# Moving vector work between the steps of a software pipeline: sums, gathering, statistics and one matrix product in a four-layer graph network

## The chip, the cores and the metric

The kernel runs on one core of one Trainium2 chip. The core has a matrix engine (PE, with its weight loads shown apart as PEld), a vector engine (DVE), an activation engine (ACT), GpSimd (POOL) and a queue engine for transfers (SP); they run at the same time and wait for each other through semaphores. The metric is the device time of one execution in microseconds (us). Three runs before the change took 1749.77, 1753.45 and 1761.13 us; the median, 1753.45 us, is the time to compare with.

## The reference

There are 128 small graphs of 64 nodes with 128 features each, and a weighted adjacency matrix `adj` of 64 x 64 for each graph. Four layers follow each other, and each is `x = layernorm(x + layer(x, adj))`.

Layers 0 and 1 are filter layers. For each edge they expand the distance into Gaussians, send them through a small network and multiply the result with the features of the neighbour, summed over the neighbours. Then come two dense layers with a shifted softplus (ssp) between them:

```python
# layer 0 (layer 1 differs in the Gaussians, the cut-off and the second ssp's place)
f_ij = jnp.exp(coeff * diff * diff)
y = x @ w_in2f
W = ssp(f_ij @ fw1 + fb1) @ fw2 + fb2
W = W * rcut[..., None]
agg = jnp.einsum('bjf,bijf->bif', y, W)
out = ssp(agg @ ow1 + ob1) @ ow2 + ob2
```

Layers 2 and 3 are graph convolutions: `norm_A @ (h @ W)` with a normalised adjacency matrix, two of them with elu in layer 2 and one with relu in layer 3.

## The kernel before

The adjacency matrices are sparse, so the kernel first sorts each graph's rows by their number of entries and packs the entries into slots of fixed sizes. This "gathering" is long: it finds the entries of each row with MAX8, FIND_INDEX8 and MATCH_REPLACE8 on DVE, and most of it runs beside layer 0, as the queue `early` (lines 1148 to 1155 and 1174).

**The main loop.** Two graphs make a pair; there are 64 pairs, and for two layers 128 turns `n`. Each turn is cut into three chunks of slots, `k` = 0, 1, 2, so the loop has 3 x 128 + 2 steps `i`. One step does, for three chunks at different stages:

- `filter_in` of this step's chunk: the product `px` on PE (L1708), then two activations into `h` on ACT (both L936).
- `filter_out` and `message` of the chunk of two steps ago: the products `pw` on PE (L1721), two of them in the only two buffers there are, and then two messages `m = (pw + bias) * g` on DVE (L1749). The next step's `pw` must wait for these two messages.
- `gather` of the chunk of one step ago: the product `pg` with the one-hot matrix on PE (L1734), and its copy `g` on ACT.
- when `k` = 0, the one-hot matrix of the turn (`hot`, L1693), one long DVE instruction.

**Sums.** After a turn's third message the generator `slot_sums` adds the slots of each row: seven reductions at L1773, each followed by a `yield`, and two at L1777 after them. The third message of a turn is made in the step with `k` = 1 of the next turn, so the sums stand in the steps with `k` = 2, 0 and 1 that follow, and have ended before that step's node work is placed.

**Node work.** Four pairs make a group (GS = 4). When a group's sums are done, its chain `node_after` is put into the queue `nodes`, and every step takes one piece of it. The pieces are: in layer 0 the share of the empty slots (`zero_share`), then the product `u` of the sums with the first dense matrix on PE (L1503); on ACT the activations Abs, Exp and Ln of `na`; on DVE `nh = max(u + bias, 0)` (L1511), `bk` (L1516) and the addition of `na` (L1519); the product `o` (L1523), its copy, the product `back` that restores the order of rows (L1532), the addition to x (L1536), and `layernorm` (L1354). A `yield True` says that a product has been put into PSUM; the rest of its piece then follows in the same step. In the layernorm BATCH_NORM_STATS2 and BATCH_NORM_AGGREGATE (L1359, L1360) run once for each of the four pairs on DVE, one small DVE instruction follows (L1362), and in the next step POOL makes the power and the scaling. In layer 1 the group's graph convolutions follow in one of two queues `convs`, eighteen steps or so each, with two further layernorms. Every full group comes in 12 steps; the last pairs of layer 1 are small groups with queues of their own, so that the end is short.

**Order.** Nothing is reordered later: `in_order` gives PE, ACT, DVE, POOL and SP the order in which the program names the instructions. On an engine everything in a step waits for what was named before it. In a step DVE has first the sums, then the gathering, the one-hot if `k` = 0, the node work, the first convolution's pieces as they come, and the messages.

The lines that drive it are

```python
        run(sums, 3)
        run(early, 9 if i < 18 else PACE if i < 3 * (NP - 8) else 7)
```

with PACE = 4 and NP = 64; `run(queue, n)` takes n pieces from a queue.

Of the kernel before, what the change touches and what calls it, by code (L numbers as in the profile page):

```python
# [601 lines left out]
def sparse_stack(ctx: ExitStack, tc: tile.TileContext, t: dict, out: bass.AP, flag):  # L602
# [14 lines left out]
    NP = NB // 2  # L617
    GS = 4
    PACE = 4
# [156 lines left out]
    def run(queue, n):  # L776

        held = None
        while queue and n:
            try:  # L780
                held = next(queue[0])
                n -= 1
            except StopIteration:
                queue.popleft()
        return held
# [139 lines left out]
    def act(out_, in_, func, **kw):  # L925
        nonlocal fence, latest, kind
        now = func == AF.Sin
        if kind is None or now != kind:
            fence = latest
            if not now:  # L930
                ctx_ = tc.issue_after(fence.ins) if fence is not None else nullcontext()
                with ctx_:
                    fence = nc.scalar.preload_act_table_set("natural_log_exp_and_others")
            kind = now
        with tc.issue_after(fence.ins) if fence is not None else nullcontext():
            latest = nc.scalar.activation(out_, in_, func, **kw)  # L936
        return latest
# [393 lines left out]
    def bank(name, n=GS):  # L1331
        ps = ps_n.tile([P, 512], F32, tag="n", name=name)[:, 0 : n * P]
        return ps, ps.rearrange("p (s c) -> p s c", s=n)

    def by_pair(v):
        return v.rearrange("p (s c) -> p s c", c=P)
# [11 lines left out]
    def once(name, n, q):  # L1348

        if n < GS and rings:  # L1350
            return tiled(name, n, q)
        return node.tile([P, GS * P], F32, tag=name, name=f"{name}_{q}", bufs=1)[:, 0 : n * P]

    def layernorm(y, dst, n, name):  # L1354

        stats = node.tile([P, GS, 6], F32, tag="st", name=f"st_{name}")[:, 0:n]
        mv = node.tile([P, GS, 2], F32, tag="mv", name=f"mv_{name}")[:, 0:n]
        for s in range(n):
            nc.vector.bn_stats(stats[:, s, :], y[:, s, :])  # L1359
            nc.vector.bn_aggr(mv[:, s, :], stats[:, s, :])  # L1360
        rstd = node.tile([P, GS], F32, tag="rs", name=f"rs_{name}")[:, 0:n]
        nc.vector.tensor_scalar(rstd, mv[:, :, 1], LN_EPS, None, ALU.add)  # L1362
        yield
        if n == GS:
            nc.gpsimd.tensor_tensor(rstd, rstd, neg_half[:, 0:n], ALU.pow)  # L1365
        else:
            act(rstd, rstd, AF.Ln)
            act(rstd, rstd, AF.Exp, scale=-0.5)
        for s in range(n):
            (nc.gpsimd if n == GS else nc.vector).tensor_scalar(  # L1370
                dst[:, s, :], y[:, s, :], mv[:, s, 0:1], rstd[:, s : s + 1],
                ALU.subtract, ALU.mult,
            )
        yield
# [81 lines left out]
    def zero_share(q, agg):  # L1456

        n = agg.shape[1]
        rows = zero_rows.pop(q)
        for b in range(2):  # L1460
            at = slice(b * A, (b + 1) * A)
            nc.vector.tensor_scalar(zblk[at, :, at], rows[at], 0.0, None, ALU.is_equal)
        yield
        _, ps = bank(f"zT_{q}", n)
        for s in range(n):
            nc.tensor.transpose(ps[:, s, :], zblk[:, s, :], ident)
        yield True
        zt = by_pair(once("zt", n, q))
        act(zt, ps, AF.Copy)
        yield  # L1470
        _, ps = bank(f"zs_{q}", n)
        y = feats[0, q]
        for s in range(n):
            nc.tensor.matmul(ps[:, s, :], lhsT=y[:, s, :], rhs=zt[:, s, :], start=True, stop=True)
        yield True
        nc.vector.scalar_tensor_tensor(agg, ps, zero_filter, agg, ALU.mult, ALU.add)
        yield
# [15 lines left out]
    def node_after(layer, q, agg):  # L1493


        w = layers[layer]
        name = f"{layer}_{q}"
        n = agg.shape[1]
        codes = node_codes.pop((layer, q))
        if layer == 0:  # L1500
            yield from zero_share(q, agg)
        u, _ = bank(f"u_{name}", n)
        nc.tensor.matmul(  # L1503
            u, lhsT=w["o1"], rhs=agg.rearrange("f s r -> f (s r)"), start=True, stop=True
        )
        yield True
        a = once("na", n, q)
        act(a, u, AF.Abs, bias=w["c1"])
        act(a, a, AF.Exp, scale=-1.0)
        h = once("nh", n, q)  # L1510
        nc.vector.tensor_scalar(h, u, w["c1"], 0.0, ALU.add, ALU.max)  # L1511
        yield
        act(a, a, AF.Ln, scale=0.5, bias=half)

        back = once("bk", n, q)
        nc.vector.tensor_scalar(back, codes, row[:, 0:1], None, ALU.is_equal)  # L1516
        back = by_pair(back)
        yield
        nc.vector.tensor_add(h, h, a)  # L1519
        yield  # L1520
        _, ps = bank(f"o_{name}", n)
        for s in range(n):
            nc.tensor.matmul(  # L1523
                ps[:, s, :], lhsT=h[:, s * P : (s + 1) * P], rhs=w["o2"], start=True, stop=True
            )
        yield True
        o = by_pair(once("no", n, q))
        act(o, ps, AF.Copy)
        yield
        _, ps = bank(f"back_{name}", n)  # L1530
        for s in range(n):
            nc.tensor.matmul(ps[:, s, :], lhsT=back[:, s, :], rhs=o[:, s, :], start=True, stop=True)  # L1532
        yield True
        y = by_pair(once("ny", n, q))
        xs = x_all[:, GROUPS[layer][q], :]
        nc.vector.tensor_add(y, ps, xs)  # L1536
        yield
        yield from layernorm(y, xs, n, name)
        if layer == 1:
            if n < GS:  # L1540
                yield from graph_convs(q)
            else:
                convs[q % 2].append(graph_convs(q))
# [241 lines left out]
    befores, nodes, convs, sums = deque(), deque(), (deque(), deque()), deque()  # L1785
# [36 lines left out]
    early = deque([gathering()])  # L1822
# [28 lines left out]
    for i in range(3 * N + 2):  # L1851
        n, k = divmod(i, 3)
        c, c1, c2 = None, *past
        run(sums, 3)
        run(early, 9 if i < 18 else PACE if i < 3 * (NP - 8) else 7)
        run(side, 1)
        run(stores, 1)
        if i == 3 * (NP + 5):
            assert not early and not side and not convs[0], "edges are still to be gathered"
            compacting.close()  # L1860
            rings.append(ctx.enter_context(tc.tile_pool(name="srings", bufs=4)))
            for q in (0, 1, *small_groups):
                group = GROUPS[1][q]
                blocks[q] = rings[0].tile(
                    [P, group.stop - group.start, P], F32, name=f"blocks{q}", bufs=1
                )
                nc.gpsimd.memset(blocks[q], 0.0)

            small[2] = by_pair(node.tile([P, GS * P], F32, tag="zt", name="small2", bufs=1))
            small[3] = zblk  # L1870
        if n < N:
            layer, p = pair_at(n)
            q = next(q for q, group in enumerate(GROUPS[layer]) if group.start <= p < group.stop)
            c = dict(
                id=f"{n}_{k}", n=n, k=k, s=p - GROUPS[layer][q].start, at=(layer, q), w=layers[layer],
                size=CHUNKS[layer][p // 8],
            )
            if k == 0:
                if n + GS < N:
                    ahead(n)  # L1880
                if n + 2 < N:
                    slot_data[n + 2] = loads(n + 2)
                if c["s"] == min(2, len(range(NP)[GROUPS[layer][q]]) - 1):
                    load_nodes(layer, q)
                if n > 0:
                    one_hot(n)
                if layer == 1 and c["s"] == 0 and q in last:
                    last[q].append(normals_of(q))
            filter_in(c)
        slot(nodes)  # L1890
        if k == 1 and befores:
            slot(befores)
        for queue in last.values():
            slot(queue)
        if c2 is not None:
            filter_out(c2)
            message(c2)
        if convs[0]:
            slot(convs[0])
        if k < 2 and n + 1 < N:  # L1900
            gaussians(n + 1, k)
        if c1 is not None:
            gather(c1)
        slot(convs[1])
        for queue in last.values():
            slot(queue)
        past = [c, c1]
# [53 lines left out]
```

## Time and profile before

| what | value |
|---|---|
| time, median of three | 1753.45 us |
| span of the profiled execution | 1760.8 us |
| PE busy | 1546.0 us, 88% |
| weight loads busy | 802.9 us, 46% |
| DVE busy | 1536.1 us, 87% |
| ACT busy | 1358.7 us, 77% |
| POOL busy | 737.7 us, 42% |
| one-hot matrices (L1693) | 128 of 1382 ns |
| reductions of the sums (L1773, L1777) | 896 of 411 ns, 256 of 368 ns |
| messages (L1749) | layer 0: 384 of 565 ns, layer 1: 384 of 628 ns |
| statistics (L1359, L1360) | 256 of 267 ns, 256 of 182 ns |
| product `u` in layer 1 (L1503) | 36 instructions of 692 ns |
| mean granted clock of PE | 0.957 |

"Busy" is the time in which an engine works on at least one instruction. The profile shows each instruction's start and length, and for an idle stretch before it, which engine's instruction ended it. In a list of waits a line reads: who waited, for whom, us in total, how many times, the longest. A timeline line reads: start in us from the span's beginning, duration, engine, line, operation, what is written and read, shapes, count, and in brackets the idle time before it and what ended it. The granted clock is the share of full speed that PE was given.

### The profile page before, as it was taken

How to read it: one execution, taken by the hardware profiler on the slowest of the kernel's cores; microseconds unless marked ns; L12 is line 12 of the kernel's file. 1: busy time of each engine (PE TensorE's matmuls, PEld its weight loads, DVE VectorE, ACT ScalarE, POOL GpSimd, SP SyncE). 2: the span in 40 equal slices, each digit the busy share in tenths (PEclk: the TensorE clock that was granted, in tenths of full speed). 3: DMA queues.
4: the chain of work that ended last, by engine and by line, in shares of the span. 5: the costliest groups of instructions: out<-in, count | busy, mean ns of one | idle time of the engine just before them, and what ended most of it. 6: DMA issues, size and time to landing. Idle time of an engine off the chain costs nothing.

```text
span 1760.8 us, 24324 instructions
## 1 busy us (share of the span) xinstructions
PE 1546.0 (88%) x6812; PEld 802.9 (46%) x6812; DVE 1536.1 (87%) x4485; ACT 1358.7 (77%) x1699; POOL 737.7 (42%) x1150
## 2 busy tenths in 40 slices
PE   1288999999989898989999989999899998999975
PEld 1133444444444444545445545455454554544444
DVE  6699899999999898888888889888898888989775
ACT  1287798888878787869999878878788787888731
POOL 2356454536556432335122354333444334534333
PEclk9998899999989898999999999999999999999986
DMA  4365456354545443336665445544454444555300
GB/s 147 84 156 130 107 127 155 106 143 105 147 108 138 108 121 94 106 82 150 153 144 121 118 108 139 121 115 113 108 134 112 117 110 103 134 125 120 75 1 21
DMA packets 112658, 202.86 MB, mean 115 GB/s; under 512 B 47214, under 2 KB 63872, under 8 KB 112384
## 3 DMA queue, kind: packets, MB, share of 16 engines
q1 hardware_dynamic: 99856, 185.24, 43.5%
q0 software_dynamic: 8080, 14.47, 2.8%
q10 hardware_dynamic: 4576, 1.49, 0.3%
q8 instruction: 56, 0.92, 0.2%
q14 instruction: 90, 0.74, 0.2%
HBM read 186.66 MB, written 14.45 MB: 114 GB/s over the span
## 4 chain that ended last, share of the span: by engine, by line
PE 47%; DVE 32%; DMA 7%; issue 5%; ACT 4%; POOL 2%; SPq 1%; DVEq 0%; ACTq 0%; POOLq 0%
PE pw L1721 17%; PE pg L1734 9%; PE px L1708 7%; DVE m L1749 7%; DVE agg L1773 6%; DVE hot L1693 4%; DMA w<-w_dram 2%; DMA d<-d_dram 2%; PE o L1523 2%; ACT h L936 2%; DVE st L1359 2%; PE y L1395 2%; PE back L1532 1%; DVE mv L1360 1%; DVE agg L1777 1%
## 5 line engine op out<-in xcount | busy, mean ns | idle before, releaser
L936 ACT ACTIVATE g<-pg 128x672 f32<-128x672 f32 (+12 forms) x384 | 299.4, 780 | 151.4 <-PE pg L1734 147.0
L936 ACT ACTIVATE h<-h,half 128x672 f32<-128x672 f32 (+13 forms) x385 | 351.2, 912 | 12.5
L1734 PE MATMUL pg<-hot,ys 64*128 64x336 f32 (+12 forms) x1536 | 351.2, 535 | 0.4 <-DVE hot L1693 0.3
L1773 DVE TENSOR_REDUCE agg<-m 128x16 f32<-128x240 f32 (+13 forms) x896 | 325.3, 411 | 2.5
L1721 PE MATMUL pw<-h,w_L_gnn_W2T 128*128 128x420 f32 (+5 forms) x768 | 310.3, 527 | 4.4 <-DVE m L1749 4.4
L1721 PE MATMUL pw<-h,w_L_gnn_fw 128*128 128x336 f32 (+6 forms) x768 | 279.7, 489 | 37.2 <-DVE m L1749 36.5
L1365 POOL TENSOR_TENSOR rs<-rs,neg_half 128x4 f32<-128x4 f32 x61 | 63.1, 1035 | 447.1 <-DVE rs L1362 447.0
L1749 DVE SCALAR_TENSOR_TENSOR m<-pw,c_L_gnn_b,g 128x420 f32<-128x420 f32 (+5 forms) x384 | 229.2, 628 | 19.6 <-PE pw L1721 13.3
L936 ACT ACTIVATE h<-px,c_L_gnn_b 128x840 f32<-128x840 f32 (+5 forms) x192 | 177.3, 924 | 61.3 <-PE px L1708 61.3
L1749 DVE SCALAR_TENSOR_TENSOR m<-pw,c_L_gnn_fb,g 128x336 f32<-128x336 f32 (+6 forms) x384 | 201.9, 565 | 25.0 <-PE pw L1721 24.1
L1708 PE MATMUL px<-d,fw 32*128 32x336 f32 (+6 forms) x768 | 169.9, 519 | 43.8 <-ACT d L936 29.9
L1734 PEld LDWEIGHTS pg<-hot,ys 64*128 64x128 f32 x1536 | 118.5, 189 | 181.7 <-ACT h L936 93.3
L1721 PEld LDWEIGHTS pw<-h,w_L_gnn_fw 128*128 128x128 f32 x768 | 139.1, 200 | 135.4 <-DVE m L1749 89.2
L1721 PEld LDWEIGHTS pw<-h,w_L_gnn_W2T 128*128 128x128 f32 x768 | 133.6, 194 | 134.7 <-DVE m L1749 40.9
L1693 DVE SCALAR_TENSOR_TENSOR hot<-j,row,w 128x1212 f32<-128x1212 bf16 (+12 forms) x128 | 176.9, 1382 | 11.1 <-DMA w<-w_dram 11.1
L936 ACT ACTIVATE h<-px,c_L_gnn_fb 128x672 f32<-128x672 f32 (+6 forms) x192 | 158.3, 825 | 15.3 <-PE px L1708 8.3
L1708 PE MATMUL px<-d,w1t 64*128 64x420 f32 (+5 forms) x768 | 169.4, 518 | 0.0
L936 ACT ACTIVATE d<-d,neg_off 128x1212 f32<-128x1212 f32 (+12 forms) x128 | 136.3, 1065 | 6.4 <-DMA d<-d_dram 6.4
L1708 PEld LDWEIGHTS px<-d,fw 32*128 32x128 f32 x768 | 60.1, 190 | 138.9 <-ACT h L936 44.6
L1008 POOL DMA_INDIRECT rows<-comb,goes x64 | 65.1, 1017 | 124.3 <-DMA rows<-comb,goes 92.7
L1008 POOL DMA_INDIRECT out_dram<-gz,at_row x56 | 62.8, 1122 | 105.1 <-DMA out_dram<-gz,at_row 95.9
L1370 POOL TENSOR_SCALAR x_all<-ny,mv,rs 128x128 f32<-128x128 f32 x124 | 97.0, 788 | 3.4
(255 smaller groups left out, 2297.0 us busy)
## 6 DMA issues: line engine op xcount, KB each, us to landing
d<-d_dram SPq DMA_DIRECT2D x32, 315.0 KB
w<-w_dram SPq DMA_DIRECT2D x32, 315.0 KB
d<-d_dram SPq DMA_DIRECT2D x32, 303.0 KB
w<-w_dram SPq DMA_DIRECT2D x32, 303.0 KB
w<-w_dram SPq DMA_DIRECT2D x32, 252.0 KB
j<-j_dram SPq DMA_DIRECT2D x32, 157.5 KB
j<-j_dram SPq DMA_DIRECT2D x32, 151.5 KB
d<-d_dram SPq DMA_DIRECT2D x16, 300.0 KB
```

The lines of the kernel that those rows point to most:

```text
L936: latest = nc.scalar.activation(out_, in_, func, **kw)
L1008: nc.gpsimd.indirect_dma_start(out=into, out_offset=bass.IndirectOffsetOnAxis(ap=at, axis=0), in_=rows, in_offset=None,)
L1359: nc.vector.bn_stats(stats[:, s, :], y[:, s, :])
L1365: nc.gpsimd.tensor_tensor(rstd, rstd, neg_half[:, 0:n], ALU.pow)
L1370: (nc.gpsimd if n == GS else nc.vector).tensor_scalar(dst[:, s, :], y[:, s, :], mv[:, s, 0:1], rstd[:, s : s + 1], ALU.subtract, ALU.mult,)
L1395: nc.tensor.matmul(ps[:, s, :], lhsT=xt[:, s * P : (s + 1) * P], rhs=w["win"], start=True, stop=True)
L1693: nc.vector.scalar_tensor_tensor(hots[n][:, 0:size], j[:, 0:size], near, wt[:, 0:size], ALU.is_equal, ALU.mult)
L1708: nc.tensor.matmul(ps[:, b, 0:n], lhsT=w["w1"][rows, :], rhs=d[rows, col : col + n], start=True, stop=True,)
L1721: nc.tensor.matmul(ps[:, 0 : c["size"]], lhsT=c["w"]["w2"], rhs=c["h"][:, b, :], start=True, stop=True)
L1734: nc.tensor.matmul(ps[:, b, 0:n], lhsT=y[rows, :], rhs=hots[c["n"]][rows, at], start=True, stop=True,)
L1749: nc.vector.scalar_tensor_tensor(messages[n][:, b, at], c["pw"][b][:, 0:size], c["w"]["b2"], c["g"][:, b, :], ALU.add, ALU.mult,)
L1773: nc.vector.tensor_reduce(av[:, :, :, r], both, AX.X, ALU.add)
```

## The change

The change removes and adds no computing. It shifts work between steps so that the step with the one-hot matrix (`k` = 0) has less other work on DVE, and so that a product isn't asked for in the step in which its input ends:

- of the sums' pieces, 1, 4 and 4 are taken when `k` is 0, 1, 2, where 3 were taken in each;
- of the gathering's pieces, 2, 5 and 5, where 4 were taken in each, in most of layer 0;
- in a layernorm of a whole group a `yield` stands after the second pair's statistics, so they are spread over two steps;
- in layer 1 a whole group's chain begins with a `yield`, so that `u` and all after it come one step later. In layer 0 `zero_share` stands there already.

```diff
@@ layernorm @@
         for s in range(n):
             nc.vector.bn_stats(stats[:, s, :], y[:, s, :])
             nc.vector.bn_aggr(mv[:, s, :], stats[:, s, :])
+            if s + 1 == GS // 2 < n:
+                yield
@@ node_after @@
         if layer == 0:
             yield from zero_share(q, agg)
+        elif n == GS:
+            yield
         u, _ = bank(f"u_{name}", n)
@@ the main loop @@
         n, k = divmod(i, 3)
         c, c1, c2 = None, *past
-        run(sums, 3)
-        run(early, 9 if i < 18 else PACE if i < 3 * (NP - 8) else 7)
+
+
+        run(sums, (1, 4, 4)[k])
+        run(early, 9 if i < 18 else (PACE - 2, PACE + 1, PACE + 1)[k] if i < 3 * (NP - 8) else 7)
         run(side, 1)
```

## The prediction

> **What bounds the kernel now.** I read the page first: busy shares, then the chain that ended last.
>
> ```profile
> PE 1546.0 (88%) x6812; PEld 802.9 (46%) x6812; DVE 1536.1 (87%) x4485; ACT 1358.7 (77%) x1699; POOL 737.7 (42%) x1150
> PE 47%; DVE 32%; DMA 7%; issue 5%; ACT 4%; POOL 2%; SPq 1%; DVEq 0%; ACTq 0%; POOLq 0%
> ```
>
> Two engines are equally busy and the chain changes between them, so hand-overs set the time. Next, busy time by stage. The timeline gives the borders: the first pair of messages (L1749) ends at 91 us, the last of layer 0 at 837, the last of layer 1 at 1702.
>
> ```profile
> 91.00:837.00 746.00, 681.08 (x2957) 336.92 (x2955) 684.89 (x2387) 619.62 (x816) 360.68 (x555) 0.95 0.49 123
> 837.00:1702.00 865.00, 810.19 (x3652) 427.61 (x3649) 751.76 (x1703) 709.85 (x829) 330.45 (x373) 0.98 0.49 116
> 1702.00:1760.80 58.80, 33.35 (x144) 25.35 (x142) 37.98 (x131) 8.56 (x31) 19.60 (x24) 0.67 0.05 16
> ```
>
> Columns are PE, PEld, DVE, ACT and POOL busy, then the granted clock and DMA. Layer 0 has 192 steps of 3.9 us with DVE 92% busy; layer 1 has 192 of 4.5 us with DVE 87%. DVE idles 61 us in layer 0 and 113 us in layer 1. DMA share is 0.49, no bound. Who waits, first in layer 0, then in layer 1:
>
> ```profile
> PE pw L1721 <- DVE m L1749: 36.5, 38, 3.6
> DVE m L1749 <- PE pw L1721: 23.6, 24, 3.9
> ```
>
> ```profile
> DVE nh L1511 <- ACT na L936: 37.6, 18, 3.0
> PE u L1503 <- DVE agg L1777: 36.3, 17, 3.3
> ```
>
> In layer 0, PE and DVE wait for each other around `pw` and the messages. In layer 1 one place dominates: PE waits for the last sums, and DVE then waits in `nh`. It recurs once a group; here, at 1208 us:
>
> ```profile
> 1207.82 0.69 DVE L1777 TENSOR_REDUCE agg<-m 128x8 f32<-128x272 f32 x2
> ...
> 1208.56 1.13 PE L1503 MATMUL u<-agg,w_L_gnn_Wd1T 128*128 128x512 f32 x2 [1.80 <-DVE agg L1777]
> ...
> 1209.73 0.69 ACT L936 ACTIVATE na<-u,c_L_gnn_bd 128x512 f32<-128x512 f32 x1 [1.00 <-PE u L1503]
> ...
> 1210.45 0.75 DVE L1511 TENSOR_SCALAR nh<-u,c_L_gnn_bd 128x512 f32<-128x512 f32 x1 [1.94 <-ACT na L936]
> ```
>
> Sums end, then `u`, then Abs, then `nh`: a serial loop through three engines, in which DVE, the fullest engine, is idle for 1.94 us and everything behind it on PE (`y`, `pw`) is late. From the ends of the message pairs in the timeline, the step with `u` takes 7.9 us on average where the mean is 4.5; DVE works 4.9 us in it.
>
> The other burst, in layer 0, is a step k = 0 with the one-hot and a whole layernorm's statistics:
>
> ```profile
> 506.76 1.26 DVE L1693 SCALAR_TENSOR_TENSOR hot<-j,row,w 128x1008 f32<-128x1008 bf16 x1
> 507.94 0.29 DVE L1359 BATCH_NORM_STATS2 st<-ny 128x6 f32<-128x128 f32 x1
> ...
> 509.66 0.17 DVE L1362 TENSOR_SCALAR rs<-mv 128x4 f32<-128x4 f32 x1
> 509.74 1.04 DVE L1749 SCALAR_TENSOR_TENSOR m<-pw,c_L_gnn_fb,g 128x336 f32<-128x336 f32 x2
> ```
>
> The messages stand behind 3 us of other work, and the next `pw` on PE then waited 1.89 us for them. Last, the clock before and at a `u` stall:
>
> ```profile
> 1140.00:1152.00 12.00, 10.52 (x53) 5.84 (x53) 9.79 (x25) 8.76 (x11) 0.20 (x1) 1.00 0.34 83
> 1152.00:1159.00 7.00, 5.60 (x14) 3.58 (x15) 2.54 (x6) 3.55 (x5) 5.04 (x6) 0.54 0.58 123
> ```
>
> The clock falls to 0.54 where PE stalls for `u` (its product starts at 1153.4). By the clock's record, layer 1 spends 27 us at half clock, 20.5 us of it in four places that begin within 1.1 us of a `u`; layer 0 spends 78.5 us so, for instance just after the burst at 510.9 us.
>
> **What the Trainium skill says.** "Perfetto Trace Analysis", Identifying the Most-Contended Engine, calls matmul busy time a bad measure and points to weight-load busy time. Agrees: PE 88% stands beside PEld 46%, so I treat DVE as the throughput bound and PE as the one whose stalls hurt. "PSUM — Partial Sum Buffer", PSUM bank collisions, has two engines kept off one bank and quadrant, reads included: that is why `nh` waits for Abs though both only read `u`. The 1.94 us agree. "TensorE: Matmul & The Clock Gate", Part 1, says the clock falls to half after a window of too little PE activity. Agrees with the 0.54. The same part, in its architectural detail, gives VectorE a strict first-in first-out queue: what stands ahead of the messages delays them. Agrees with the burst.
>
> **The change part by part.** It adds and removes no work: every matmul, activation and DVE instruction is still there once.
>
> (1) *Sums.* Nine reductions a pair (seven L1773, two L1777) stood 3, 3, 3 over k = 2, 0, 1; now 4, 1, 4. The step of the one-hot has two reductions fewer: 325.3 us / 896 = 0.36 us each, 0.7 us. The sums still end in k = 1.
>
> (2) *Gathering.* 4, 4, 4 becomes 2, 5, 5 nearly to layer 0's end. These are mostly MAX8, FIND_INDEX8 and MATCH_REPLACE8 of about 0.21 us: 0.4 us off k = 0.
>
> (3) *Statistics.* Four pairs of L1359 and L1360 take 1.72 us (507.94 to 509.66); 0.86 us moves on by a step. In layer 0 the statistics fall in k = 0, the second half now in k = 1.
>
> Together, in layer 0 (loads summed from the timeline): DVE has 4.3, 2.9 and 3.5 us in k = 0, 1, 2, mean 3.5. After: 4.3 - 0.5 (layer 0's reductions are shorter, 0.27 us) - 0.4 - 0.2 (0.86 once in four) = 3.2; 2.9 + 0.3 + 0.2 + 0.2 = 3.6; 3.5 + 0.3 + 0.2 = 4.0. The spread nearly halves. DVE's 23.6 us of waiting for `pw` is the gain available, and PE's 36.5 us its cause; between none and all of it, I take half: 12 us.
>
> (4) *`u` a step later in layer 1.* PE no longer waits for sums that ended a step ago. `nh` still waits for Abs, which on ACT stands behind the step's Exp and Ln, but four reductions (1.4 us) are ahead of it. The nearest row is layer 0, where sums are likewise long done at `u`: `nh` idles 11.4 us in 15 groups, 0.76 us each. Layer 1 idles 34.7 / 17 = 2.04 us. The difference, 1.28 us, times 15 full groups is 19 us. Bounds: zero, if the wait moves whole, and 35 us.
>
> (5) *Clock.* At half clock PE needs about 6.4 us for a layer 0 step that lasts 3.9 (3.2 us of matmuls at full speed, an estimate from start-to-start times in the timeline), so such stretches lose about 0.39 of their length: 30 us in layer 0. In layer 1 (8 us against 4.5) the four stalls lose 9 us. Part of that is the waits already counted. I take 8 and 5 us; bounds 0 and 39.
>
> (6) *What the delay costs.* The wait added is one of position: each node chain of layer 1 ends two steps later, each graph convolution takes two more. The chain then has 9 of a group's 12 steps (layer 0: 11), a convolution 20 of its 24, so neither queues. Three layernorms a group share two statistics buffers, each now held a step longer, about three steps of twelve; DVE waited for POOL here only 1.0 us. But two convolutions of four pairs run about four steps further into the tail of 58.8 us, whose own chain is the last pair's. Eight such pieces at 0.4 us, half of the DVE row of 0.6 to 0.7 us, partly in that chain's waits: +3 us, bounds 0 and 8.
>
> Sum: -12 - 19 - 8 - 5 + 3 = -41; 1753 - 41 = **1712 us**.
>
> **Rivals.** *The waits move.* DVE's total is unchanged and PE, ACT and DVE differ by little a step, so a stall removed at `u` returns at `nh`, `gy_hw` or `em`. For: DVE's small waits for PE in the convolutions (`gy_hw` 11.1, `em` 8.5, `gz` 8.2 us) are untouched. Against: `u` is one place with a cause of its own. A quarter of the gains, 11 us, less 3: 1745 us.
>
> *Slower.* Four reductions now stand ahead of everything else in k = 1 and k = 2, and in layer 1 the shifted pieces meet: the step two after the new `u` gets two activations' halves (1.3 us), half a statistics and the reductions, about 5.2 us on DVE. If PE stalls there 1.5 us a group in 16 groups, that is 24 us, with the tail at 8 and the gains of layer 0 at 12: 1753 + 24 + 8 - 12 = 1773 us. Against: layer 1 already has steps with 6.2 us of DVE work, and PE waits only 4.4 us for messages there.
>
> *More.* Nearly all of it: 20 + 30 + 25 = 75 us, 1678 us. For: stalls and half clock feed each other.
>
> **How the numbers follow.** Forecast 0.55, waits move 0.22, slower 0.12, more 0.11. One per cent is 17.5 us, so faster means below 1736. The forecast with its bounds falls there nine times in ten; so 0.49 + 0.02 + 0.11 gives faster 0.62, same 0.25, slower 0.13. The range is 1680 to 1760: it leaves out most of the slower case and the end of "more".
>
> **What would show it.** Right: `u` <- sums nearly gone in layer 1; `nh` <- Abs near 15 us; `pw` <- messages below 20 us in layer 0; fewer half-clock stretches, page clock from 0.957 to 0.97. The prediction is wrong if `nh` or the copies in the convolutions wait as long as `u` did, if half clock stays, or if the last stretch grows past 65 us.

## The result and the profile after

| what | before | after |
|---|---|---|
| time, median of four runs each | 1757.29 us (1749.77 to 1762.16) | 1710.61 us (1702.35 to 1715.96) |
| ratio after to before, 95% interval | | 0.9734 (0.9677 to 0.979) |
| layer 0, first to last pair of messages | 743.5 us | 740.4 us |
| layer 1, to its last pair of messages | 867.9 us | 818.8 us |
| what follows the last messages | 58.5 us | 64.1 us |

The kernel is 2.7% faster. The stages come from the two profiles, with borders taken exactly at the ends of the message pairs (the prediction put the border between the layers at 837 us, one pair of messages late; layer 0's last pair ends at 834.4 us). They differ by -3, -49 and +6 us. So the gain lies in layer 1, and the tail gives some of it back; the 3 us of layer 0 are within the scatter described below.

The page of the kernel after, its busy shares and the shares of the chain that ended last:

```profile
PE 1534.4 (90%) x6812; PEld 796.3 (46%) x6812; DVE 1529.9 (89%) x4485; ACT 1355.5 (79%) x1699; POOL 753.1 (44%) x1150
PE 31%; DVE 25%; issue 15%; DMA 12%; POOL 11%; ACT 4%; SPq 2%; DVEq 0%; POOLq 0%; ACTq 0%
```

The counts are those of before, and the busy times too, within 1% on the four engines but POOL (2% more): the same work in less time. The mean clock rose only from 0.957 to 0.96. The same stages as before, again PE, PEld, DVE, ACT and POOL, then clock and DMA:

```profile
91.00:831.00 740.00, 675.17 (x2950) 333.96 (x2946) 682.46 (x2380) 619.88 (x813) 360.57 (x552) 0.95 0.47 123
831.00:1650.00 819.00, 800.02 (x3651) 421.78 (x3651) 745.55 (x1701) 705.10 (x830) 339.86 (x372) 0.99 0.51 122
1650.00:1714.07 64.07, 37.75 (x150) 27.60 (x149) 40.32 (x139) 9.91 (x33) 25.79 (x30) 0.63 0.05 14
```

Layer 0 has the clock it had, 0.95, and DVE is 92% busy in it, as before. Layer 1 went from DVE 87% to 91% and from 0.98 to 0.99. Its time at half clock, by the clock's record, is 14 us where it was 34 (the 27 us of the prediction leave out two stretches of 3.4 us near the layer's end). The waits of the kernel after, in us, times and the longest; first layer 0:

```profile
PE pw L1725 <- DVE m L1753: 47.6, 49, 3.1
DVE m L1753 <- PE pw L1725: 21.7, 17, 4.2
```

PE waits more for the messages than before (36.5 us). Layer 1:

```profile
DVE nh L1515 <- ACT na L936: 32.5, 18, 3.2
...
DVE m L1753 <- PE pw L1725: 8.8, 13, 1.3
...
DVE gz L1669 <- PE o L1666: 3.7, 6, 0.7
...
PE u L1507 <- DVE agg L1781: 3.7, 2, 3.1
...
DVE gy_hw L1612 <- PE hw L1609: 2.7, 7, 0.5
```

PE's stop at `u` has gone: 3.7 us in two places instead of 36.3 in 17. The wait of `nh` has hardly changed, 32.5 us after 37.6. What did shrink is not in the forecast's sum: DVE's waits for PE's products in the convolutions and the restored rows (`gy_hw`, `em`, `gz`, `gy_sup`, `nTs`, `ny` together) fell from 44.3 to 15.3 us. The three largest of them were, before the change:

```profile
DVE gy_hw L1608 <- PE hw L1605: 11.1, 14, 1.3
...
DVE em L1549 <- PE gh L1635: 8.5, 14, 1.1
DVE gz L1665 <- PE o L1662: 8.2, 13, 1.1
```

In layer 1 DVE idles 73.5 us instead of 113.5, and PE 19.0 us instead of 54.8.

Why `nh` still waits is in the timeline of the kernel after at a `u` of layer 1:

```profile
1186.88 1.13 PE L1507 MATMUL u<-agg,w_L_gnn_Wd1T 128*128 128x512 f32 x2
...
1187.74 0.93 ACT L936 ACTIVATE h<-px,c_L_gnn_b 128x800 f32<-128x800 f32 x1
1188.70 0.96 ACT L936 ACTIVATE h<-h,half 128x800 f32<-128x800 f32 x1
1189.57 0.67 ACT L936 ACTIVATE na<-u,c_L_gnn_bd 128x512 f32<-128x512 f32 x1
1190.27 0.75 DVE L1515 TENSOR_SCALAR nh<-u,c_L_gnn_bd 128x512 f32<-128x512 f32 x1 [1.80 <-ACT na L936]
```

`u` now starts without a wait and ends at 1188.0, but Abs stands behind the step's Exp and Ln on ACT and starts at 1189.57, and `nh` behind Abs. The prediction knew this queue, and took the four reductions ahead of `nh` to cover all but 0.76 us of the wait.

### The profile page after: what moved, and what is told of

Same layout as the page of the kernel before. It is cut to its first block, busy times and chain, and to the rows that moved or that the text cites. A ratio compares the mean times of both kernels' runs of the same rounds, so it can differ in the third digit from the quotient of the medians.

```text
span 1714.1 us, 24319 instructions
## 1 busy us (share of the span) xinstructions
PE 1534.4 (90%) x6812; PEld 796.3 (46%) x6812; DVE 1529.9 (89%) x4485; ACT 1355.5 (79%) x1699; POOL 753.1 (44%) x1150
## 4 chain that ended last, share of the span: by engine, by line
PE 31%; DVE 25%; issue 15%; DMA 12%; POOL 11%; ACT 4%; SPq 2%; DVEq 0%; POOLq 0%; ACTq 0%
PE pw L1725 11%; DMA out_dram<-gz,at_row 7%; DVE m L1753 6%; PE pg L1738 6%; PE px L1712 6%; POOL x_all L1372 4%; DVE agg L1777 4%; POOL rs L1367 2%; DMA w<-w_dram 2%; DVE hot L1697 2%; POOL gz L1372 2%; ACT h L936 2%; DVE at L1151 2%; DMA d<-d_dram 1%; SPq L1246 1%
## 5 line engine op out<-in xcount | busy, mean ns | idle before, releaser
L936 ACT ACTIVATE h<-h,half 128x672 f32<-128x672 f32 (+13 forms) x385 | 351.1, 912 | 12.5
L1725 PE MATMUL pw<-h,w_L_gnn_fw 128*128 128x336 f32 (+6 forms) x768 | 279.1, 488 | 47.7 <-DVE m L1753 47.6
L1725 PE MATMUL pw<-h,w_L_gnn_W2T 128*128 128x420 f32 (+5 forms) x768 | 304.8, 520 | 3.0 <-DVE m L1753 3.0
L1367 POOL TENSOR_TENSOR rs<-rs,neg_half 128x4 f32<-128x4 f32 x61 | 68.6, 1125 | 282.7 <-DVE rs L1364 281.3
L1372 POOL TENSOR_SCALAR x_all<-ny,mv,rs 128x128 f32<-128x128 f32 x124 | 108.9, 884 | 3.4
L1008 POOL DMA_INDIRECT out_dram<-gz,at_row x56 | 71.9, 1283 | 52.4 <-DMA out_dram<-gz,at_row 39.4
```

Source lines behind the costliest of these rows:

```text
L1008: nc.gpsimd.indirect_dma_start(out=into, out_offset=bass.IndirectOffsetOnAxis(ap=at, axis=0), in_=rows, in_offset=None,)
L1372: (nc.gpsimd if n == GS else nc.vector).tensor_scalar(dst[:, s, :], y[:, s, :], mv[:, s, 0:1], rstd[:, s : s + 1], ALU.subtract, ALU.mult,)
L1725: nc.tensor.matmul(ps[:, 0 : c["size"]], lhsT=c["w"]["w2"], rhs=c["h"][:, b, :], start=True, stop=True)
```

## The experiments

My theory after the result: in layer 1 the delay of `u` does everything, and the rest of the change does nothing. Its rivals were that the evenly spread sums and statistics bring the gain, and that it isn't the stop at `u` but the new places of the pieces behind it. The table has every run; time is the ratio to the kernel before in rounds on the same chip, and the other columns are us in one profile of the run. "Half clock" counts each stretch whole, in the stage in which it begins. "Conv" is the sum of DVE's waits for PE just named.

| run | ratio (95%) | layer 0 | layer 1 | tail | half clock L0, L1 | L1: `u` | `nh` | conv |
|---|---|---|---|---|---|---|---|---|
| before | 1 | 743.5 | 867.9 | 58.5 | 78.5, 34.1 | 36.3 | 37.6 | 44.3 |
| after | 0.9734 (0.9677 to 0.979) | 740.4 | 818.8 | 64.1 | 75.1, 13.7 | 3.7 | 32.5 | 15.3 |
| e1, `u` late alone | 0.9685 (0.9649 to 0.9721) | 734.5 | 804.0 | 64.0 | 54.6, 0 | 3.6 | 20.2 | 11.2 |
| e2, sums alone | 0.992 (0.989 to 0.995) | 740.9 | 851.0 | 59.3 | 85.3, 30.7 | 32.7 | 38.5 | 34.6 |
| e3, statistics alone | 0.9912 (0.9877 to 0.9947) | 739.1 | 843.4 | 61.1 | 71.7, 13.7 | 29.1 | 36.6 | 34.4 |
| e4, gathering alone | 0.9997 (0.9977 to 1.0017) | 733.2 | 868.3 | 57.9 | 54.6, 30.7 | 36.3 | 37.7 | 44.1 |
| e5, places behind `u` alone | 0.9865 (0.9824 to 0.9906) | 741.0 | 829.3 | 64.0 | 68.3, 17.1 | 14.1 | 38.9 | 16.5 |
| e6, `u` late, rest in place | 0.9841 (0.9796 to 0.9886) | 730.5 | 839.0 | 59.9 | 61.4, 10.2 | 4.8 | 28.1 | 35.6 |
| e8, after, `nh` before Abs | 0.9713 (0.967 to 0.9756) | 733.0 | 815.5 | 63.6 | 75.1, 10.2 | 3.7 | 1.5 | 38.3 |
| e9, before, `nh` before Abs | 0.998 (0.9956 to 1.0005) | 740.7 | 865.4 | 58.5 | 68.3, 27.3 | 36.3 | 23.9 | 44.4 |
| e10, e1 and e2 | 0.9683 (0.9636 to 0.9729) | 766.6 | 805.3 | 63.9 | 109.2, 3.4 | 3.6 | 14.8 | 17.2 |
| e11, e1 and e3 | 0.977 (0.9726 to 0.9813) | 761.6 | 823.7 | 64.1 | 99.0, 3.4 | 3.5 | 36.8 | 14.1 |
| e12, `u` late but for the last two groups | 0.9716 (0.9674 to 0.9758) | 768.9 | 814.2 | 58.4 | 105.8, 6.8 | 6.5 | 24.1 | 12.5 |
| e13, e12 and e9 | 0.9645 (0.9604 to 0.9686) | 771.8 | 808.9 | 59.5 | 109.2, 3.4 | 6.5 | 5.6 | 16.5 |

Two cautions on reading it. The programs of before, e1, e5 and e6 are identical through layer 0 and gave 743.5, 734.5, 741.0 and 730.5 us: one profile's layer 0 is known to about 6.5 us either way. Layer 1 repeats far better: before and e4, with the same program there, took 867.9 and 868.3 us. And e10 to e13 ran on another chip, on which the kernel before took 1793.45 us in the median, against 1754.04 us for e1 to e4 and 1753.22 us for e5 to e9; only their ratios and their layer 1 are set beside the others. Layer 1 may be: e1 and e12 have the same program in its first 168 of 192 steps, and took 693.8 and 694.3 us for them on the two chips.

**The parts, each alone on the kernel before (e1 to e4).**

```diff
 # e1, in node_after
+        elif n == GS:
+            yield
 # e2
-        run(sums, 3)
+        run(sums, (1, 4, 4)[k])
 # e3, in layernorm, after bn_aggr
+            if s + 1 == GS // 2 < n:
+                yield
 # e4
-        run(early, 9 if i < 18 else PACE if i < 3 * (NP - 8) else 7)
+        run(early, 9 if i < 18 else (PACE - 2, PACE + 1, PACE + 1)[k] if i < 3 * (NP - 8) else 7)
```

> The one-step delay of u in layer 1 alone. If the stop of PE at u is what cost time, nearly all of layer 1's gain of 46 us is here: layer 1 near 825 us, PE's wait for the last sums gone, ratio about 0.975. If the new shares of sums and statistics made the gain in layer 1, this run stays within 10 us of before (ratio 0.995 or more). Layer 0 unchanged in both (near 744 us).

> The sums alone at 1, 4, 4. If u's stop is the cause, layer 1 stays within 10 us of before, since u still waits for the last sums in its own step; ratio 0.99 to 1.005. If unloading the one-hot's step is the cause, layer 1 loses 20 us or more. In layer 0: between 0 and -10 us.

> The statistics in two steps alone. They take 0.86 us out of a burst of 3 us in layer 0's step with the one-hot; if such bursts cost time, layer 0 loses about 5 to 10 us; if DVE's total is what counts there, nothing. In layer 1 within 10 us of before either way, as u's stop stays. Ratio 0.99 to 1.0.

> The gathering alone at 2, 5, 5. Touches layer 0 alone. If it takes load off the step that holds PE back, layer 0 loses 3 to 8 us; if it only moves the burst to the steps k = 1 and 2, nothing or up to 5 us slower. Layer 1 unchanged. Ratio 0.995 to 1.003.

Measured: e1 alone gives 0.9685, all of the full change's gain (the two intervals overlap). Its layer 1 is even shorter, 804.0 us, and has no half clock at all. The stage of layer 1 in e1, in the same columns, and its largest waits of DVE there:

```profile
825.00:1629.00 804.00, 793.90 (x3654) 420.81 (x3653) 741.58 (x1705) 707.30 (x830) 325.44 (x376) 1.00 0.52 125
```

```profile
DVE nh L1513 <- ACT na L936: 20.2, 16, 3.1
DVE m L1751 <- PE pw L1723: 18.3, 17, 1.5
DVE gy_hw L1610 <- PE hw L1607: 4.9, 8, 0.7
```

PE is busy for 794 of 804 us; DVE's waits for it in the convolutions are nearly over.

e2 and e3 each gain 0.8 to 0.9%, which my theory missed, and they gain it in the wrong layer for the prediction: 17 and 25 us of layer 1, and 3 and 4 us of layer 0, which is within its scatter. Their `u` stops are shorter, 32.7 and 29.1 us, and the convolutions' waits fall by 10 us in both. e4 does nothing, 0.9997 with 0.002 either way. Multiplied, the four parts would give 0.952; the full change gives 0.9734. So the gains do not add.

**Stop or place? (e5, e6).** The added `yield` does two things: `u` comes a step after its sums, and all that follows it moves by a step against the sums, the one-hot matrix and the layernorms. e5 leaves `u` where it was and shifts only what follows its first piece; e6 delays `u` and joins two later pieces, so that the product `o` and everything behind it stay where they were.

```diff
 # e5, after the piece with nh
         yield
+        if layer == 1 and n == GS:
+            yield
 # e6: e1, and ahead of the addition of na
-        yield
+        if layer == 0 or n < GS:
+            yield
         nc.vector.tensor_add(h, h, a)
```

> From the kernel before: u keeps its step in layer 1, and the added step stands just after its piece, so that all later pieces of a full group stand where the change puts them. If u's stop is the cause, the wait of PE for the last sums stays near 36 us and little is gained (ratio 0.99 or more). If the new places of the later pieces are the cause, the gain of the one-step delay appears here without it (ratio about 0.98).

> From the kernel before: u one step later in layer 1, and two later pieces of the chain joined (the addition of na follows in the step of bk), so that o and all after it stand where they stood. If u's stop is the cause, the gain stays, layer 1 near 830 us, ratio about 0.98. If the places of the later pieces are the cause, none is left, ratio 0.995 or more.

Measured: 0.9865 and 0.9841. In layer 1 e5 saves 39 us, e6 29 us, and e1, which does both, 64. So the new places gain by themselves, with `u` in its old step, and so does the later `u` by itself. Waits in layer 1 of e5:

```profile
DVE nh L1511 <- ACT na L936: 38.9, 16, 3.0
...
PE u L1503 <- DVE agg L1779: 14.1, 17, 2.9
```

And in layer 1 of e6, those of DVE and one of PE:

```profile
DVE nh L1513 <- ACT na L936: 28.1, 18, 3.1
DVE gy_hw L1611 <- PE hw L1608: 11.1, 14, 1.3
DVE gz L1668 <- PE o L1665: 8.2, 13, 1.1
DVE m L1752 <- PE pw L1724: 7.3, 10, 1.5
...
PE o L1526 <- DVE nh L1522: 15.7, 15, 1.3
```

In e5 `u` still waits in all 17 places, but only 14.1 us instead of 36.3, and the convolutions' waits are 16.5 us. A reason can be read in the timeline of before: at the `u` of 1208 us a convolution's layernorm has its statistics from 1205.0 to 1206.9 us, behind the one-hot matrix and ahead of the last three reductions. With the copy behind them that is 2.5 us. At the same `u` in e5 (1191 us) two other instructions stand there, 1.3 us in all, and `u` waits 0.54 us instead of 1.80.

In e6 `u` waits 4.8 us, but the convolutions' waits are 35.6 us, not far below the 44.3 of before. So it is the new places, and not the missing stop, that bring most of these waits down. The stop itself was worth less than its length in e6 because part of it came back: PE now waits 15.7 us at `o` for the sum `nh`, where it waited 3.1 us before. At one such place (1198 us) DVE has this sum directly behind the one-hot matrix, and PE, no longer stopped at `u`, idles 0.90 us at `o`.

By step, the mean length in layer 1 for `k` = 0, 1, 2 is 5.37, 4.38, 3.82 us before, 4.59, 4.69, 3.68 in e5, 5.34, 3.54, 4.23 in e6 and 4.56, 4.03, 3.97 in e1. The new places take 0.8 us off the step with the one-hot matrix, the later `u` takes 0.8 us off the step in which it stood, and each gives some of it back in another step. The two runs do not split the gain cleanly: e5 shortens the stop too, by 22 us, and in e6 some 13 us of it return at `o`.

**The wait of `nh` (e8, e9).** `nh` and Abs both read `u`; written first, `nh` no longer stands behind ACT's queue. e8 makes the exchange in the kernel after, e9 in the kernel before.

```diff
-        act(a, u, AF.Abs, bias=w["c1"])
-        act(a, a, AF.Exp, scale=-1.0)
         h = once("nh", n, q)
         nc.vector.tensor_scalar(h, u, w["c1"], 0.0, ALU.add, ALU.max)
+        act(a, u, AF.Abs, bias=w["c1"])
+        act(a, a, AF.Exp, scale=-1.0)
```

> The changed kernel with the two readers of u in the other order: nh on DVE first, then Abs on ACT. DVE's wait for Abs, 32.5 us in layer 1 and 13.6 us in layer 0 of the changed kernel, should go; ACT gets Abs up to 1 us later, which it can bear. If DVE's idle time at nh is on the path, 15 to 30 us less than the changed kernel: 1685 to 1695 us, ratio to before 0.96 to 0.965. If PE and ACT bound layer 1 by now, the wait moves and the time stays near 1710 us.

> The same exchange in the kernel before. PE's stop at u stays (36 us), but nh no longer waits for Abs behind it: 0.7 us a group in layer 1 and 0.8 us in layer 0 at most, some 20 us together. If PE's stop is what costs, the gain is 5 to 12 us, ratio 0.993 to 0.997; if DVE's idle time is what costs, about 20 us, ratio 0.988.

Measured: 0.9713 and 0.998, both within their intervals of the kernels that they change. The waits of DVE in layer 1 of e8:

```profile
DVE gz L1669 <- PE o L1666: 15.2, 13, 1.7
DVE gy_hw L1612 <- PE hw L1609: 13.0, 20, 1.2
DVE m L1753 <- PE pw L1725: 8.6, 13, 1.3
```

Here a removed wait did move: `nh` went from 32.5 to 1.5 us, and `gz`, `gy_hw` and the like rose from 15.3 to 38.3. DVE's idle time in layer 1 fell by under 4 us. My reading is that, while DVE stood at `nh`, PE got ahead and had the later products ready, and that without this pause DVE meets them unfinished. In e9 there was less to win than I expected: `nh` no longer waited for Abs, but 23.9 us for `u` itself, and DVE's wait for `pw` at the messages grew from 13.3 to 23.4 us.

**Which part spoils e1? (e10, e11).** The full change has three parts more than e1 and gains no more.

> The one-step delay of u together with the sums at 1, 4, 4. The delay alone gave 0.9685, the sums alone 0.992. If they act on different waits, the two multiply: 0.961. If both relieve the same stop before u, nothing is added: 0.968. If the new sums are what spoils the delay in the full change, 0.973 or more, with layer 1 near 815 us instead of 804.

> The one-step delay of u together with the statistics in two steps. Alone they gave 0.9685 and 0.9912; if they multiply, 0.960; if both relieve the same stop, 0.968; if the statistics' extra step moves the convolutions to worse places and spoils the delay, 0.973 or more, with layer 1 near 815 us and a longer end (65 us or more).

Measured: 0.9683 with the sums, nothing added; 0.977 with the statistics, slower than e1 with intervals that just do not overlap (0.9721 and 0.9726), and measured on another chip. The plainer sign is layer 1, which repeats between the chips: it takes 823.7 us to e1's 804.0, and `nh` waits 36.8 us to 20.2. Besides the wait, DVE itself works longer. The timeline of e11 shows one place:

```profile
1300.60 1.46 DVE L1364 TENSOR_SCALAR rs<-mv 128x4 f32<-128x4 f32 x1
...
1300.74 1.28 POOL L1393 TENSOR_TENSOR x_all<-x_all,b_L_gnn_bd 128x512 f32<-128x512 f32 x1
```

The small instruction behind the statistics, 0.17 us in the median, took 1.46 us and ended with POOL's addition (1302.06 and 1302.02 us). All 70 of its kind take 12.0 us in e1 and 24.7 us in e11. In layer 1 of the kernel before and of the kernel after, in count, busy us, mean ns and idle us before it, the group is

```profile
L1362 DVE TENSOR_SCALAR rs<-mv 128x4 f32<-128x4 f32 (+1 forms) x44 | 8.8, 200 | 1.5
```

```profile
L1364 DVE TENSOR_SCALAR rs<-mv 128x4 f32<-128x4 f32 (+1 forms) x43 | 13.4, 312 | 1.5
```

The second half of the statistics comes a step later and now meets POOL's work. From e1 to the kernel after, layer 1 grows by 14.8 us: DVE idles 11.1 us more, while its wait at `nh` alone grows by 12.3, and it works about 4 us more, while these instructions alone grow by 5.9 (7.5 to 13.4). That accounts for it, but why `nh` waits longer I did not isolate.

**The tail (e12, e13).** The delay is left out for the last two groups (`elif n == GS and q < 13`); e13 also has the exchange of e9.

> The delay of u for the full groups but the last two of layer 1, whose convolutions run into the end. If the 5.5 us by which the last stretch grew come from those two groups, the end returns to about 59 us and the ratio goes from 0.9685 to about 0.966; layer 1 loses up to 3 us of its gain. If not, the end stays at 64 us.

> The run before this, with nh on DVE ahead of Abs on ACT. With the full change the exchange took 31 us of DVE's waits at nh away and gave them back as waits of the convolutions, at a gain of 0 to 6 us. If that holds in general, the ratio stays within 0.003 of the run before this one; if the waits come back only because of where the convolutions stand in the full change, up to 20 us less, ratio 0.956.

Measured: the tail is back at 58.4 us, but the ratio, 0.9716, is no better than e1's: layer 1 took 814.2 us, 10 us more than in e1 where I had expected 3 at most. All but about half a us of that arises in the last 24 steps, in which the chains of the last two groups run, so they cost more than the tail gets back. With the exchange, e13 reaches 0.9645 (0.9604 to 0.9686), the smallest ratio of all, which the exchange on its own (e9) did not foretell; why it gains here is open. It is 0.7 points below e12, and the two intervals just overlap; so do those of e13 and the full change, by 0.0009. e13 is thus the best candidate, not a proven winner over e1.

## Why the prediction was right, and where its sum was wrong

The forecast of 1712 us fell on the measured time, but by luck: two errors cancelled in its sum. Its -41 us were -20 in layer 0 (12 and 8), -24 in layer 1 (19 and 5) and +3 in the tail. The profiles show -3, -49 and +6, so 17 us too much was forecast for layer 0 and 25 us too little for layer 1.

- **Steps (1) to (3), -12 us in layer 0: wrong.** The loads moved as worked out, but the long step moved with them: mean lengths for `k` = 0, 1, 2 went from 4.45, 3.57, 3.65 to 3.47, 4.19, 3.97 us, with the mean at 3.89 and 3.88. The step that failed is "the spread nearly halves" taken as a gain. My loads after, 3.2, 3.6 and 4.0, left out that the two steps with more work get the messages late in their turn; PE's wait for them rose to 47.6 us, where I had said below 20. With DVE at 92%, I take what counts in layer 0 to be its total, which no part changes; no run tests this by itself. e4 alone shows the gathering's share as nothing.
- **Steps (1) and (3) in layer 1: not priced.** I counted them in layer 0 only. Alone they save 17 and 25 us of layer 1 (e2, e3); beside the delay of `u`, none (e10) or less than none (e11).
- **Step (4), -19 us for `u`: right in the stop, wrong in the term.** The stop went as forecast, from 36.3 to 3.7 us, and e6 shows its removal, with what that brings back at `o`, to be worth 29 us of layer 1. But I priced it through `nh`, as 1.28 us times 15 groups, and that wait fell by 5 us only. At 32.5 us it is nearly as long as the stop at `u` had been, which I had named as a sign of being wrong, and far from the 15 us that I had named as a sign of being right. The nearest row that I took, `nh` in layer 0, did not carry over: Abs still queues behind Exp and Ln. What fell instead, the convolutions' waits (44.3 to 15.3 us), hangs on the places of the pieces: 16.5 us in e5, where `u` stays, and 35.6 us in e6, where they stay.
- **Step (5), half clock: half right.** In layer 1 its time fell from 34 to 14 us, and to zero in e1. PE's own busy time there fell from 813 to 800 us, of which about 5 us are work that moved into the tail; so of the 49 us the clock can explain some 8 to 13, an estimate from these figures, against the 5 that I had priced. The mean clock of the profile reached 0.96, not the 0.97 that I had named. In layer 0 it did not change beyond scatter (78.5 and 75.1 us), so the 8 us there are void, with the burst that was to go.
- **Step (6), the cost of delay: mis-sized, and with the wrong sign in layer 1.** The tail's +3 us (0 to 8) measured 5.6. But I took the later places of the pieces only as a cost. In e5 those places, with `u` kept in its step, save 39 us of layer 1, partly by shortening the stop at `u`.
- **The rivals.** "The waits move" was right about `nh`, and e8 shows such a move plainly, but the convolutions' waits fell instead of growing. "Slower" had PE stalling in the steps that the shifted pieces share; PE's idle time in layer 1 fell by two thirds. "More" was right that stalls and half clock go together in layer 1, and wrong on layer 0.

What stays open: which of the shifted places of e5 is worth most, how the gain of e1 divides between stop and places, and why the statistics' split lengthens the wait of `nh` beside a late `u`.

## What to carry to other kernels

In a pipeline whose order is written out, one added wait of position moves everything behind it against everything else, so price the new places as well as the removed stop, and try the parts alone and in pairs: here one part gave all of the gain, and another took some back. After removing a stop, add up all waits of both engines, not only the one next to it: here the wait next to it hardly fell, others fell far more, and in e6 over a third of the stop came back at another product. Evening out the load of the steps brought nothing measurable in layer 0, where DVE was already 92% busy over all of them.

## What the runs showed of the hardware

- A DVE instruction on 128 x 4 elements took 1.46 us instead of 0.17 while POOL added two tiles in SBUF, and ended with it. All ten of its kind in e11 that took over 0.6 us ended within 0.04 us after an addition of POOL. The Trainium skill, "SBUF — State Buffer", Who interferes with whom, says that VectorE and GpSimd share one pair of ports and that this is an exclusive lock; the trace agrees, and it costs 12.7 us of DVE time in e11 against e1.
- Half clock in the midst of dense work: before the change the four stretches of layer 1 named in the prediction began within 1.1 us of a stop of 2.9 to 3.3 us at `u`. Two other stops there of 2.7 and 2.9 us and six of 1.8 us began none, and in e5 three stretches began where PE had no stop above 1.4 us, so the length of one stop does not decide it. Without the stops (e1) layer 1 had none, at PE busy 99%.
- The chip of e10 to e13 ran the kernel before 2% slower. Its layer 0 took 762 to 772 us with 99 to 109 us at half clock, where the other profiles had 730 to 744 us with 55 to 85; layer 1 was the same to within 0.5 us where the programs agree (e1 and e12, above). What makes the chips differ was not tried.
